# A cross-attention kernel on one core: in the last batch product 4's right sums go ahead of block 12; in the first batch several sums, two pairs of scores and T4 are moved

## The chip, the core and the metric

The kernel runs on one core of one Trainium2 chip. Five engines work side by side, each through its own list of instructions in order: TensorE (PE, the matmuls), VectorE (DVE), ScalarE (ACT), GpSimd (POOL) and SyncE (SP). DMAs are issued from the lists of SP, ACT and POOL; an issue that has to wait for a semaphore stands in its list like any other instruction. The metric is the time of one execution on the device in microseconds (us), lower is better.

## The reference, cut to what matters

Eight batches. In each, x1 and x2 are 512 channels by 1024 positions, all float32:

```python
q = einsum('bcn,dc->bnd', x1, Wq) + bq            # d = 64
k = einsum('bcn,dc->bdn', x2, Wk) + bk[:, None]
v = einsum('bcn,dc->bdn', x2, Wv) + bv[:, None]
attn = softmax(einsum('bnd,bdm->bnm', q, k), axis=2)
out = einsum('bcm,bnm->bcn', v, attn) + x1
```

## The kernel before

**The algebra.** With e the exponentials of the scores less their maximum and den their sums, the output is Wv (x2 e) / den + bv + x1. Per batch the kernel makes Y = x2 e (512 x 1024 times 1024 x 1024), scales it by 1/den, makes Wv Y, and adds bias and x1. Both big products are cut in 2 x 2 blocks and done with seven block products instead of eight. The left factor x2 gives blocks a11, a12, a21, a22 and the left sums S1 (of a21 and a22), S2 (of a11 and S1), S3 (of a11 and a21, written over a21) and S4 (of a12 and S2); the right factor e gives blocks 11, 12, 21, 22 and the right sums T1 (of 12 and 11), T2 (of T1 and 22), T3 (of 22 and 12, written over 12) and T4 (of 21 and T2). The signs stand in `left_sums` (L101) and `right_sums` (L259). The table `MULT` (L298 on) says which factors each product takes: 1: a11 and block 11; 2: a12 and 21; 6: S2 and T2; 7: S3 and T3; 5: S1 and T1; 3: S4 and 22; 4: a22 and T4. Some of the products, 3 and 4 in every batch, are cut in seven once more, by `inner_left` (L349), `inner_right` (L358) and `multiply_onto` (L422); for product 4 the four inner right sums are made by `inner_right(s, 4, ...)`, four VectorE instructions, and the inner products that need them come second and later.

**Tiles.** Positions (the contraction of the first product) lie on the 128 partitions. A right block holds 4 tiles of 128 x 512; query halves 0 and 1 are `s.e[0]` and `s.e[1]`. `scores(s, h, i)` makes one pair of score tiles (one of each half of the keys) for half h, and ScalarE copies them from PSUM to SBUF. Then VectorE folds the maximum over the four pairs (`fold`), GpSimd reduces it over the partitions (`highest`, PARTITION_ALL_REDUCE, top), VectorE subtracts (L243 in the head, L249 elsewhere), ScalarE exponentiates, VectorE folds the sum and GpSimd reduces it (`total`, den). Its reciprocal is taken on a small copy (`few`) and sent back through DRAM (`shares`).

**The order.** It is written out by hand: the program is recorded under a manual schedule, so that each engine's list is in the order of the source. `head` (L609) and `head_second` (L685) are the start of batch 0; `period(s, n, nn, nnn)` (L708) is batch s, with the scores and projections of the next batch n and the loads for the two batches after it woven in. `nn` is the batch after next: in `period` of batch 0 its queries are projected (`queries(nn)`, PE L149 ps_q) right after the scores of half 0 of batch 1.

**The loads on SP.** `load_x` (L122) loads x1 or x2 of a batch in four DMAs of 512 KB into one buffer (tag x). `load_a` (L128) loads a block of x2 transposed; the tiles a11 and a12 have one buffer each, a21 and a22 two (`bufs=1 + (k[0] == "2")`, L131). A load into a buffer waits until the last reader of the tile that lay there is done, and SP issues in the order of the list. In the first batch that list reads, after the loads of the head: x1 of batch 1, x2 of batch 1 (after its queries), a11 of batch 1 (L732), x1 of batch 2 (L737, after the keys of batch 1), a21 and a22 of batch 1, x2 of batch 2. The readers of batch 0's a11 are product 1 on TensorE and the sums S2 and S3 on VectorE.

**The first batch around the change.** `head` makes, in order: the scores of half 0, their maximum; S1 and S2 on VectorE while GpSimd reduces; three pairs of scores of half 1; the eight subtractions and exponentials of half 0; three folds of its sum. `period` runs product 1, then `head_second`: fourth pair, the rest of the maximum of half 1, the queries of batch 1, S3 and S4 while GpSimd reduces, the exponentials of half 1. Then T1 and T2, the reduction of sum 0, product 2, the keys of batch 1, `sum_t4` (L271; in batches 0 and 1 two VectorE additions, from batch 2 on two ScalarE copies and two accumulating DMAs of POOL), the sum of half 1, T3, product 6, the scores and queries that belong to the next batches, products 5, 7, 3, 4.

**The last batch around the change.** After product 7, `multiply_3(s, hooks[1])` makes product 3 onto bank a; `evict_y(s, "22", (1,))` completes block 22; `evict_3()` adds the inner terms and completes block 12 (three VectorE instructions: `complete`, then two additions from PSUM); `inner_right(s, 4, ...)` makes the inner right sums of product 4; then the blocks are scaled by 1/den, and `multiply_4` follows.

Of the kernel before, what the change touches and what calls it, by code (L numbers as in the profile page):

```python
# [11 lines left out]
ALU = mybir.AluOpType  # L12
# [3 lines left out]
def kernel(  # L16
# [53 lines left out]
    MH = N // P // 2  # L70
# [64 lines left out]
    def sum_a(s, *ks):  # L135
        for k in ks:
            if k != "S3":
                s.a[k] = sb.tile([P, MH, C // 2], F32, tag=f"a{k}", name=f"a{k}_{s.b}")
        left_sums(s.a, *ks)
# [35 lines left out]
    def scores(s, h, i, bank=None):  # L175


        if i == 0:
            s.e[h] = sb.tile([P, 2, MH, H], F32, tag=f"e{h}", name=f"e_{s.b}_{h}")
        e = s.e[h]  # L180
        if bank:
            whole = None
            ps = [
                ps_a.tile([P, H], F32, tag=f"{bank}{g}", name=f"ps_s{bank}{g}_{s.b}_{h}_{i}")
                for g in range(2)
            ]
        else:
            whole = ps_s.tile([P, 2, H], F32, tag="sc", name=f"ps_s_{s.b}_{h}_{i}")
            ps = [whole[:, g, :] for g in range(2)]
        for g, r in ((0, lo), (1, hi)):  # L190
            nc.tensor.matmul(  # L191
                ps[g], s.k[r, ts(i, P)], s.q[r, ts(h, H)], start=True, stop=True
            )

        def copy():
            if bank:
                for g in range(2):
                    nc.scalar.copy(e[:, g, i, :], ps[g])
            else:
                nc.scalar.copy(e[:, :, i, :], whole)  # L200

        copy.ps = ps
        return copy

    def fold(s, h, i, kind, op):

        e = s.e[h]
        if i == 1:
            s.mx[h] = sb.tile([P, 2, H], F32, tag="fold", name=f"{kind}_{s.b}_{h}", bufs=2)
        f = s.mx[h]  # L210
        nc.vector.tensor_tensor(f, e[:, :, 0, :] if i == 1 else f, e[:, :, i, :], op)  # L211
# [59 lines left out]
    def sum_t4(s):  # L271

        s.t["T4"] = t4 = sb.tile([P, MH, H], F32, tag="eT4", name=f"eT4_{s.b}")
        if s.b < 2:
            sum_e(s, "T4")
            return
        for i in (0, 2):
            nc.scalar.copy(t4[:, i : i + 2, :], s.t["21"][:, i : i + 2, :])
        for i in (0, 2):
            nc.gpsimd.dma_start(t4[:, i : i + 2, :], s.t["T2"][:, i : i + 2, :], accum_op=ALU.add)  # L280
# [328 lines left out]
    def head(s):  # L609

        s.q = sb.tile([P, N], F32, tag="q", name=f"q_{s.b}", bufs=2)
        s.k = sb.tile([P, H], F32, tag="k", name=f"k_{s.b}", bufs=2)
        x1_sb = sb.tile([P, CT, N], F32, tag="x", name="x1_head")
        x2_sb = sb.tile([P, 2, MH, H], F32, tag="e1", name="x2_head")
        s.x = x2_sb.rearrange("p a (b t) n -> p (a b) (t n)", t=2)  # L620

        def load_x1(c, h):
            nc.sync.dma_start(
                x1_sb[:, c : c + 2, ts(h, H)],
                x1[s.b, c * P : (c + 2) * P, ts(h, H)].rearrange("(t p) n -> p t n", p=P),
            )

        nc.gpsimd.dma_start(bqk_sb, bqk)
        nc.gpsimd.dma_start(bv_sb, bv)
        nc.scalar.dma_start(wqk_sb, wqk)  # L630
        warm = const.tile([P, P], F32, name="warm")
        nc.vector.memset(warm, 0.0)
        ps = ps_a.tile([P, H], F32, tag="a0", name="ps_warm")
        for _ in range(WARM):
            nc.tensor.matmul(ps[:, 0:P], warm, warm, start=True, stop=True)
        load_x1(0, 0)
        load_x1(2, 0)
        for n in HALVES:
            for c in range(CT):
                to, of = (  # L640
                    x.rearrange("p (h n) -> p h n", h=2)[:, :, n]
                    for x in (s.x[:, c, :], x2[s.b, ts(c, P), :])
                )
                nc.sync.dma_start(to, of)
        nc.scalar.activation(warm[:, 0:1], warm[:, 0:1], AF.Exp)
        load_x1(0, 1)
        load_x1(2, 1)
        load_a(s, "21", "22", "11", "12")
        load_values()
        tiles = range(CT)  # L650
        head_queries(s, x1_sb, 0, "c1")(*tiles)
        head_keys(s, left, "c0")(*tiles)
        more_keys = head_keys(s, right, "a0")
        more_keys(0)
        s.mx[0] = f = sb.tile([P, 2, H], F32, tag="fold", name=f"max_{s.b}_0", bufs=2)
        copies = [scores(s, 0, i) for i in range(2)]
        for g in range(2):
            nc.scalar.copy(s.e[0][:, g, 0, :], copies[0].ps[g])
            nc.vector.tensor_tensor(f[:, g, :], s.e[0][:, g, 0, :], copies[1].ps[g], ALU.max)
        fold_halves(s, 0, ALU.max)  # L660
        more_keys(*tiles[1:])
        copies[1]()
        more_queries = head_queries(s, x1_sb, 1)
        more_queries(0)
        for i, bank in ((2, "a"), (3, "c")):
            copy = scores(s, 0, i, bank)
            for g in range(2):
                nc.vector.tensor_tensor(f[:, 0, :], f[:, 0, :], copy.ps[g], ALU.max)
            copy()
        highest(s, 0, halves=False)  # L670
        sum_a(s, "S1", "S2")
        more_queries(*tiles[1:])
        load_x(states[1], x1)
        copies = [scores(s, 1, 0), scores(s, 1, 1), scores(s, 1, 2, "c")]
        for g in range(2):
            for i in range(MH):
                first_exponentials(s, g, i)
        for copy in copies:
            copy()
        fold(s, 0, 1, "sum", ALU.add)  # L680
        fold(s, 0, 2, "sum", ALU.add)
        fold(s, 1, 1, "max", ALU.max)
        fold(s, 0, 3, "sum", ALU.add)

    def head_second(s, n):  # L685


        scores(s, 1, 3)()
        for i in range(2, MH):
            fold(s, 1, i, "max", ALU.max)  # L690
        queries(n)
        load_x(n, x2)
        highest(s, 1)
        sum_a(s, "S3", "S4")
        for i in range(MH):
            exponentials(s, 1, i)

# [10 lines left out]
    def period(s, n, nn, nnn):  # L708
# [15 lines left out]
        if s.b == 0:  # L724
            head_second(s, n)
        sum_e(s, "T1", "T2")
        if s.b < 2:
            total(s, 0)
        else:
            shares(s, 0)  # L730
        if n:
            load_a(n, "11")  # L732
        if s.b == 0:
            first(2)
            evict_y(s, "11", (1,))
            keys(n)
            load_x(nn, x1)  # L737
            sum_t4(s)
            sums(s, 1)
            shares(s, 0)  # L740
        else:
            evict = multiply_2(s)
            sums(s, 1)
            evict()
            if s.b == 1:
                shares(s, 0)
            sum_t4(s)
            sum_a(s, "S4")
# [37 lines left out]
        if seven:  # L786
            hooks = [{}, {}]
            if n:
                for i in range(MH):
                    lower(n, 0, i)  # L790
                hooks = [
                    {
                        1: lambda: copy_first(n, 0),
                        6: lambda: add_exponential(1),
                        5: lambda: add_exponential(2),
                    },
                    {6: lambda: add_exponential(3)},
                ]
            first(5, (lambda: exponential(n, 0, 0)) if n else None)
            inner_right(s, 3, s.t["22"], "eT1")  # L800
            inner_left(s, 4, s.a["22"], "a12")
            add_7 = multiply_7(s, hooks[0])
            add_7()
            evict_3 = multiply_3(s, hooks[1])
            evict_y(s, "22", (1,))
            evict_3()
            inner_right(s, 4, s.t["T4"], "eT2")
        else:
            first(5)
            if s.b == 0:  # L810
                inner_right(s, 3, s.t["22"], "eT1")
                for i in range(MH):
                    lower(n, 0, i)
            else:
                for i in range(MH):
                    exponentials(n, 0, i)
                start_sum(n, 0)
                inner_right(s, 3, s.t["22"], "eT1")
            first(7)
            if s.b > 1:  # L820
                inner_right(s, 4, s.t["T4"], "eT2")
            evict_3 = multiply_3(s, {})
            if s.b:
                evict_y(s, "22", (1,))
                evict_3()
            else:
                evict_3()
                evict_y(s, "22", (1,))
# [105 lines left out]
```

## Time and profile before

| what | value |
|---|---|
| median of 3 runs | 693.22 us (693.14 to 693.31) |
| the profiled execution's own time | 693.62 us |
| its span, first to last instruction | 691.8 us |
| PE busy | 682.8 us, 99% |
| DVE busy | 628.9 us, 91% |
| ACT busy | 276.1 us, 40% |
| POOL busy | 193.5 us, 28% |
| mean DMA rate | 158 GB/s |
| mean granted TensorE clock | 1.000 |

Times inside the execution are counted from the start of the span. A line of the timeline gives the start, the length, the engine, the line of the source, the operation, out<-in, shapes, the number of instructions merged, and in brackets the idle time of the engine before it with what ended it. "SPq", "POOLq" and "ACTq" are issues and waits in an engine's list. A matmul's length includes its pipeline; the distance from one start to the next is what it costs TensorE: 0.43 us for a matmul record of 512 columns, 0.215 us where two column groups of 64 share the array, as in the projections.

### The profile page before, as it was taken

Reading aid. Unit: us, or ns where it says so; the run is one execution under the profiler, and the core shown is the slowest. Engines: PE = TensorE matmul, PEld = TensorE weight load, DVE = VectorE, ACT = ScalarE, POOL = GpSimd, SP = SyncE. Lnnn points to the kernel's source line nnn. Section 1 sums busy time; section 2 is a strip of 40 time slices with the busy share of each in tenths; the row PEclk is TensorE's granted clock in tenths of the full one; section 3 lists DMA queues with packets and bytes.
Section 4 is the critical chain, followed back from the end, with each engine's and each line's share of the span. In section 5 each row is a group of like instructions: output and inputs, shape, how many; then the busy total and the mean of one; then the engine's idle time right before and its main releaser. Section 6 shows DMA issues by size and latency. Waiting matters only on the chain.

```text
span 691.8 us, 6647 instructions
## 1 busy us (share of the span) xinstructions
PE 682.8 (99%) x2248; PEld 364.2 (53%) x2248; DVE 628.9 (91%) x809; ACT 276.1 (40%) x439; POOL 193.5 (28%) x147
## 2 busy tenths in 40 slices
PE   9999999999999999999999999999999999999997
PEld 5333554535545565455644566454754545545753
DVE  1999999988999889998999989999799988999785
ACT  2733353146233552345432454424544245243220
POOL 0123113522423223242142321623223232323000
PEclk9999999999999999999999999999999999999999
DMA  9676256954569754786628867198642864268303
GB/s 304 258 214 238 65 182 130 255 161 79 183 114 235 199 106 153 150 231 181 135 111 180 230 181 187 42 198 215 167 92 38 207 166 76 62 148 223 87 0 122
DMA packets 44723, 109.05 MB, mean 158 GB/s; under 512 B 4880, under 2 KB 7184, under 8 KB 44688
## 3 DMA queue, kind: packets, MB, share of 16 engines
q1 hardware_dynamic: 25856, 70.13, 30.1%
q0 software_dynamic: 17424, 36.25, 29.7%
q10 hardware_dynamic: 1408, 2.23, 1.0%
q8 instruction: 18, 0.29, 0.2%
q14 instruction: 17, 0.14, 0.1%
HBM read 72.62 MB, written 16.81 MB: 129 GB/s over the span
## 4 chain that ended last, share of the span: by engine, by line
PE 93%; DMA 3%; DVE 1%; SPq 1%; ACT 1%; issue 0%; DVEq 0%
PE ps_ya L321 24%; PE ps_i L374 17%; PE ps_oa L321 16%; PE ps_oc L321 12%; PE ps_s L191 6%; PE ps_yc L374 5%; PE ps_q L149 4%; PE ps_k L149 3%; PE ps_yc L321 3%; PE ps_ya L374 3%; DMA a<-in_x2T_dram 1%; DMA x_in_x_dram<-in_x_dram 1%; DMA x_head<-in_x_dram 1%; PE ps_sc L191 1%; PE ps_sa L191 1%; DVE aS L110 0%
## 5 line engine op out<-in xcount | busy, mean ns | idle before, releaser
L321 PE MATMUL ps_ya<-eT,aS 128*128 128x512 f32 x256 | 113.1, 595 | 0.0
L332 ACT COPY uy<-ps_ya 128x512 f32<-128x512 f32 x48 | 28.1, 588 | 139.6 <-PE ps_ya L321 126.7
L249 DVE TENSOR_TENSOR e<-e,top 128x1024 f32<-128x1024 f32 x60 | 70.5, 1228 | 11.0 <-POOL top L221 11.0
L321 PEld LDWEIGHTS ps_ya<-eT,aS 128*128 128x128 f32 x256 | 48.0, 190 | 60.9 <-issue 58.5
L253 ACT ACTIVATE e<-e 128x1024 f32<-128x1024 f32 x60 | 62.9, 1059 | 38.6 <-DVE e L249 37.1
L221 POOL PARTITION_ALL_REDUCE top<-max x16 | 32.8, 2052 | 150.8 <-DVE max L215 78.9
L226 POOL PARTITION_ALL_REDUCE den<-sum x16 | 63.4, 3961 | 40.8 <-DVE sum L215 35.8
L321 PE MATMUL ps_oa<-yT,w_S 128*128 128x512 f32 x128 | 57.6, 593 | 0.0
L321 PE MATMUL ps_oc<-y,w 128*128 128x512 f32 x128 | 57.6, 593 | 0.0
L321 PE MATMUL ps_ya<-e,a 128*128 128x512 f32 x128 | 56.3, 593 | 0.3 <-ACT e L244 0.3
L200 ACT COPY e<-ps_s 128x1024 f32<-128x1024 f32 x46 | 45.7, 1027 | 19.3 <-PE ps_s L191 17.5
L332 ACT COPY uo<-ps_oa 128x512 f32<-128x512 f32 x48 | 27.6, 584 | 54.2 <-PE ps_oa L321 44.9
L383 ACT COPY d<-ps_i 128x256 f32<-128x256 f32 x84 | 29.3, 374 | 47.7 <-PE ps_i L374 47.2
L191 PE MATMUL ps_s<-q,k 64*128 64x512 f32 x188 | 47.3, 608 | 0.8 <-ACT q L590 0.8
L551 POOL DMA_DIRECT2D uo<-in_x_dram x21 | 24.9, 1186 | 79.2 <-DVE uo L548 79.2
L555 POOL DMA_DIRECT2D sum<-e x21 | 25.7, 1222 | 66.5 <-DMA sum<-e 37.0
L321 PEld LDWEIGHTS ps_ya<-e,a 128*128 128x128 f32 x128 | 24.2, 190 | 31.3 <-issue 29.6
L321 PEld LDWEIGHTS ps_oa<-yT,w_S 128*128 128x128 f32 x128 | 24.2, 190 | 30.8 <-issue 29.9
L321 PEld LDWEIGHTS ps_oc<-y,w 128*128 128x128 f32 x128 | 24.1, 190 | 31.0 <-issue 28.9
L211 DVE TENSOR_TENSOR max<-max,e 128x1024 f32<-128x1024 f32 x30 | 36.8, 1225 | 3.0
L507 DVE TENSOR_TENSOR y<-y,den 128x512 f32<-128x512 f32 x54 | 33.8, 683 | 0.0
L238 POOL DMA_DIRECT2D den<-row x16 | 8.9, 557 | 79.0 <-DMA row<-few 73.2
(142 smaller groups left out, 1291.4 us busy)
## 6 DMA issues: line engine op xcount, KB each, us to landing
x_in_x_dram<-in_x_dram SPq DMA_DIRECT2D x60, 512.0 KB, 5.9
a<-in_x2T_dram SPq DMA_DIRECT2D x32, 512.0 KB, 7.1
sum<-e POOLq DMA_DIRECT2D x21, 512.0 KB, 5.2
uo<-in_x_dram POOLq DMA_DIRECT2D x21, 512.0 KB, 6.5
out_dram<-uo SPq DMA_DIRECT2D x21, 512.0 KB, 5.1
eT<-eT POOLq DMA_DIRECT2D x12, 512.0 KB, 6.5
den<-row POOLq DMA_DIRECT2D x16, 256.0 KB, 3.6
r<-in_x_dram POOLq DMA_DIRECT2D x7, 512.0 KB, 8.6
```

The costliest lines, as they stand in the source:

```text
L149: nc.tensor.matmul(ps[r, :], w_sb[:, c, :], s.x[:, c, ts(h, H)], start=(c == 0), stop=(c == CT - 1),)
L191: nc.tensor.matmul(ps[g], s.k[r, ts(i, P)], s.q[r, ts(h, H)], start=True, stop=True)
L200: nc.scalar.copy(e[:, :, i, :], whole)
L211: nc.vector.tensor_tensor(f, e[:, :, 0, :] if i == 1 else f, e[:, :, i, :], op)
L221: nc.gpsimd.partition_all_reduce(s.top[h], s.mx[h][:, 0, :], P, ReduceOp.max)
L226: nc.gpsimd.partition_all_reduce(s.den[h], s.mx[h][:, 0, :], P, ReduceOp.add)
L249: nc.vector.tensor_tensor(e, e, top, ALU.subtract)
L253: nc.scalar.activation(e, e, AF.Exp)
L321: nc.tensor.matmul(ps[:, n], left[ka][:, k, ts(j, P)], right[kb][:, k, n], start=opens and k == 0, stop=i in (2, 3, 4) and k == n_k - 1, s ...
L332: nc.scalar.copy(s.tmp[i][:, j, :], ps)
L374: nc.tensor.matmul(ps, s.inner[i][ka][:, k, :], s.inner[i, "t"][kb][:, k, :], start=opens and k == 0, stop=z in (2, 3, 4) and k == MH // 2 ...
L507: nc.vector.tensor_tensor(y[:, j, :], y[:, j, :], rden, ALU.mult)
```

## The change

In the last batch, and only there, `inner_right(s, 4, ...)` is called before `evict_3()`.

In the first batch:

- pair 2 of the scores of half 1 leaves `head` for `head_second`, so that TensorE makes pairs 2 and 3 after product 1 (in the file before, pair 2 came ahead of it);
- S1 and S2 come after the eight subtractions of half 0 on VectorE, where they came ahead of them;
- S3 and S4 leave `head_second` for `period`, behind `shares(s, 0)`, that is behind the sum of half 1;
- of the three folds of sum 0, the last two go behind T1 and T2;
- T4 is made by two ScalarE copies and two accumulating DMAs of POOL, as in batches 2 to 7, where it was two VectorE additions. Batch 1 keeps the additions.

The source calls `load_a(n, "11")` where it did. No arithmetic is added or left out.

```diff
     def sum_t4(s):
 
         s.t["T4"] = t4 = sb.tile([P, MH, H], F32, tag="eT4", name=f"eT4_{s.b}")
-        if s.b < 2:
+        if s.b == 1:
             sum_e(s, "T4")
             return
         for i in (0, 2):
@@ head
         highest(s, 0, halves=False)
-        sum_a(s, "S1", "S2")
         more_queries(*tiles[1:])
         load_x(states[1], x1)
-        copies = [scores(s, 1, 0), scores(s, 1, 1), scores(s, 1, 2, "c")]
+        copies = [scores(s, 1, i) for i in range(2)]
         for g in range(2):
             for i in range(MH):
                 first_exponentials(s, g, i)
         for copy in copies:
             copy()
+        sum_a(s, "S1", "S2")
+        fold(s, 1, 1, "max", ALU.max)
         fold(s, 0, 1, "sum", ALU.add)
-        fold(s, 0, 2, "sum", ALU.add)
-        fold(s, 1, 1, "max", ALU.max)
-        fold(s, 0, 3, "sum", ALU.add)
 
     def head_second(s, n):
 
-        scores(s, 1, 3)()
+        copies = [scores(s, 1, 2, "c"), scores(s, 1, 3)]
+        for copy in copies:
+            copy()
         for i in range(2, MH):
             fold(s, 1, i, "max", ALU.max)
         queries(n)
         load_x(n, x2)
         highest(s, 1)
-        sum_a(s, "S3", "S4")
         for i in range(MH):
             exponentials(s, 1, i)
@@ period
         sum_e(s, "T1", "T2")
+        if s.b == 0:
+            for i in range(2, MH):
+                fold(s, 0, i, "sum", ALU.add)
         if s.b < 2:
             total(s, 0)
@@
             sum_t4(s)
             sums(s, 1)
             shares(s, 0)
+            sum_a(s, "S3", "S4")
@@
             evict_y(s, "22", (1,))
-            evict_3()
+            if n:
+                evict_3()
             inner_right(s, 4, s.t["T4"], "eT2")
+            if not n:
+                evict_3()
```

## The prediction

> **What bounds the kernel now.** The page comes first, for the bound and the chain that ended last.
>
> ```profile
> PE 682.8 (99%) x2248; PEld 364.2 (53%) x2248; DVE 628.9 (91%) x809; ACT 276.1 (40%) x439; POOL 193.5 (28%) x147
> ...
> PE 93%; DMA 3%; DVE 1%; SPq 1%; ACT 1%; issue 0%; DVEq 0%
> ```
>
> TensorE never rests for long, so a change pays only where TensorE waits, and costs only where it is made to wait. The waits of TensorE come next, the longest two:
>
> ```profile
> PE ps_i L374 <- DVE eI4eT L367: 2.3, 1, 2.3
> ...
> PE ps_s L191 <- ACT q L590: 0.8, 1, 0.8
> ```
>
> The first is in the last batch. The timelines of TensorE and VectorE there show product 4 standing still until its inner right sums (eI4eT) exist, and VectorE making block 12 (L452, L483) ahead of them.
>
> ```profile
> 655.34 1.03 PE L374 MATMUL ps_i<-eT,a 128*128 128x256 f32 x4
> 658.65 1.97 PE L374 MATMUL ps_i<-eI4eT,aI 128*128 128x256 f32 x8 [2.28 <-DVE eI4eT L367]
> ```
>
> ```profile
> 652.31 1.01 DVE L502 TENSOR_TENSOR y<-ps_yc,uy 128x512 f32<-128x512 f32 x2
> 654.49 0.69 DVE L452 TENSOR_TENSOR d<-d,v 128x512 f32<-128x512 f32 x1 [1.16 <-ACT d L383]
> 655.29 1.29 DVE L483 TENSOR_TENSOR y<-ps_ya,d 128x512 f32<-128x512 f32 x2
> 656.49 0.68 DVE L367 TENSOR_TENSOR eI4eT<-eT 128x512 f32<-128x512 f32 x1
> ```
>
> For the first batch I read SP's timeline (x2 of batch 1, a11 of batch 1, x1 of batch 2, a21 and a22), then TensorE at the queries of batch 2, which read that x1, and at product 5 behind them.
>
> ```profile
> 36.78 2.00 SPq L126 DMA_DIRECT2D x_in_x_dram<-in_x_dram  x4
> 38.82 0.78 SPq L133 DMA_DIRECT2D a<-in_x2T_dram  x1
> 48.00 1.75 SPq L126 DMA_DIRECT2D x_in_x_dram<-in_x_dram  x4
> 49.79 1.22 SPq L133 DMA_DIRECT2D a<-in_x2T_dram  x2
> ```
>
> ```profile
> 58.58 3.65 PE L149 MATMUL ps_q<-x_in_x_dram,wqk_sb 128*64 128x512 f32 x16
> 62.17 1.12 PE L321 MATMUL ps_ya<-eT,aS 128*128 128x512 f32 x2
> ```
>
> Last come VectorE and GpSimd, for the sums that move and the reductions beside them.
>
> ```profile
> 36.44 1.22 DVE L110 TENSOR_TENSOR a<-a,a 128x1024 f32<-128x1024 f32 x1
> 37.58 2.06 DVE L110 TENSOR_TENSOR aS<-a,aS 128x1024 f32<-128x1024 f32 x1
> 39.56 4.62 DVE L249 TENSOR_TENSOR e<-e,top 128x1024 f32<-128x1024 f32 x4
> ...
> 50.69 3.44 DVE L262 TENSOR_TENSOR eT<-e,eT 128x1024 f32<-128x1024 f32 x2
> ...
> 58.51 4.38 DVE L262 TENSOR_TENSOR e<-e 128x1024 f32<-128x1024 f32 x2
> ```
>
> ```profile
> 20.63 2.68 POOL L221 PARTITION_ALL_REDUCE top<-max  x1 [18.15 <-DVE max L668]
> ```
>
> ```profile
> 152.81 1.78 POOL L221 PARTITION_ALL_REDUCE top<-max  x1 [11.20 <-DVE few L234]
> ```
>
> S3 is the first line: done at 37.66, before a11's issue at 38.82. A reduction beside VectorE's 128x1024 sums takes 2.68, with VectorE idle 1.78, and it holds up one sum (2.06 for S4, 3.44 where two take 2.4).
>
> **The change part by part.** *Last batch.* The four inner sums can start when block 22's evictions end, at 653.3 (T4 landed long before). They take 0.69, 0.72, 0.61 and 0.61 (start to start); the third, which the second inner product needs, ends at 655.25. TensorE reaches that product at 655.34 + 0.86 = 656.2 and does not wait. It started at 658.65: 2.45 gained. Late next is VectorE's block 12: its three instructions start at 655.8 and end at 657.85, and the 1.24 between 659.02 and 657.78 is what VectorE gains down to block 21, scaled by 669.19 - 1.24 = 667.95; its reader, at 670.77 on TensorE, comes to 668.32. So it fits by 0.37; if not, some tenths come back. Term: -2.45 (0 if the stall only changes its name).
>
> *Scores, S1 and S2 later.* The first top reduction then runs with VectorE idle: 20.63 + 1.78 = 22.41, VectorE starts at 22.45 instead of 23.57, and product 1 at 23.84 instead of 24.96 (the 1.39 for a subtraction and an exponential kept). But the third pair, 0.86, now follows product 1 instead of filling the wait for it, so the queries of batch 1 start at 33.08 - 1.12 + 0.86 = 32.82: 0.26 earlier. x2 of batch 1 is issued when they end, so the keys and product 6 come 0.26 earlier too (47.63). S1 and S2, 2.4 behind the subtractions, end at 29.7, hidden behind product 1, whose next reader of S2 is product 6. Copies of pairs 2 and 3 on ScalarE end at 32.8 and 33.96, the maximum at 36.1; the second reduction, again alone, ends at 36.2 + 1.78 = 37.97, and the subtractions start at 38.0 instead of 39.56.
>
> *T4 on ScalarE and POOL.* Two copies (1.99 in batch 7's row) fit between the keys' activation at 48.4 and product 6's first copy at 51.4. The two DMAs stand in POOL's list behind few_0 (54.7 to 56.6 by batch 7's 1.80 for two) and ahead of the second sum's reduction (57.2): nobody waits. They land by 62 (4.6 to 6.5 us after issue in quiet stretches); the first reader is inner_right, after 65. If that cover went, product 4's 89.36 is the next limit. VectorE loses 3.36 of work (50.69 to 54.05).
>
> *Sums later, and S3.* VectorE from 38.0: subtractions, T1 and T2 take 9.33 (39.56 to 48.89), to 47.3; two folds of sum 0, 2.5, and halves, 0.7, to 50.5; block 11, 1.2, to 51.7; the first fold of sum 1 is held by the den reduction (3.24, from 50.6) to 53.9; two folds, halves and the reciprocal, 3.3, to 57.2. few_0, issued at 54.2, lands by 56.5 at its median of 2.3 us. S3 then takes 1.2: done at 58.4 instead of 37.66. T3 follows S4 and ends near 63, before product 7 (76 before).
>
> *What stands behind S3.* a11 of batch 1 overwrites the a11 that S3 reads, in its only buffer. In the built program that load waits for VectorE's 42nd signal, which is S3 (26th before, S3 again). SP issues in order, so behind it stand x1 of batch 2 (four DMAs), a21, a22. The queries of batch 2 need that x1 at 58.3, where it was issued at 48.0 and had all landed by 55.8 (the fourth issued at 49.32, landed 6.5 later). Now: a11 issued at 58.4, x1 right behind. Five loads land, by that row, the first 3.8 after issue, the fifth 1.3 after the fourth's 7.8: 9.1, so 67.5. The T4 DMAs may still be running (61.8): between 0 and 2.2 more (x2 of batch 2, issued at 62.28 beside other transfers, took 10.05 for its four instead of 7.8); 0.6 taken. Product 5 follows the last landing by 1.0 (the keys' last chunk at 46.88, product 6 at 47.88): 69.1.
>
> *The clock.* TensorE would stand from 58.3 to about 63.8. The only row of an idle TensorE is the end of the run:
>
> ```profile
> 691.60:691.80 0.20, 0.00 (x0) 0.00 (x0) 0.00 (x0) 0.00 (x0) 0.00 (x0) 0.50 0.00 0
> ```
>
> The granted clock is 0.50 there, 3.5 us after the last matmul, and the first 20 matmuls of the run (128 columns) came 0.213 us apart, as far as 256-column records stand apart later, for 4.3 us. At half speed for 4.3 us from 63.8, ten of the 16 records take 0.43 and six 0.215: 5.6 us instead of the 4.8 that the landings allow: 0.8 more. If the clock holds, 0. I take 0.4. (The Trainium skill, TensorE: Matmul & The Clock Gate, Part 1, says that the gate halves the clock after an idle window of about 3.4 us and opens after about 3.4 us of work; by it eight records are slow, 5.2 us, an estimate, 0.4 more and not 0.8. No run here shows yet which.)
>
> Sum: product 5 at 69.1 + 0.4 = 69.5 instead of 62.17, +7.3; it holds the 0.26 gained earlier. After 62 the trace shows no wait of TensorE that could give this back until 586, and that one is VectorE's, which moves along. 7.3 - 2.45 = +4.9 on the profiled execution's 693.62 (span 691.8 and 1.8 around it), which lies 0.40 above the median: 693.22 + 4.9 = 698.1.
>
> **The rivals.**
> 1. *S3 is later still.* The reduction of sum 1 starts when S3 does; T3's second half beside such a reduction took 3.26, not 1.2: +2.1. Or few_0 lands 5.9 us after issue, as its slowest did, and holds the reciprocal to 60.1: +2.9. Against: T3's first half, in just S3's place behind the reciprocal, took 1.19. 700.2 to 701.
> 2. *The loads are quicker or partly covered.* No contention, clock held, S3 0.5 earlier: 7.3 - 0.6 - 0.4 - 0.5 = 5.8, less 2.45: 696.6, and down to 695.8 if the chunks land closer together.
> 3. *SP's hold ends too early to matter: faster.* Then the last batch's 2.45 and the 0.26 remain: 690.5. Product 5 must start by 62.17 + 2.45 = 64.6 for break-even, so S3 must be done by 64.6 - 10.1 = 54.5, 3.9 before my chain. For: T4's 3.36 left VectorE. Against: it is counted already, and two folds took its place.
> 4. *The last batch gains nothing*: block 21 or the denominators become the wait. 698.1 + 2.45 = 700.5. Against: the 0.37 of room.
>
> **How the numbers follow.** My forecast 0.60 (own range 696.9 to 699.5); rival 1 0.17; rival 2 0.12; rival 3 0.05; rival 4 0.06. The predicted time is 698.1. A range from 696.4 to 700.8 leaves out rival 3, the lower half of rival 2 and the far part of rival 1, about 0.18. Within 0.2% (1.4 us, about what a measurement can tell from no change) there is only a rival 3 that half works: 0.02. Faster 0.05, slower 0.93.
>
> **What would show it.** Right: a wait of 5 to 6 us of ps_q L149 on x_in_x_dram near 58 and smaller ones between its chunks; SP's a11 issue near 58.4; S3 there on VectorE; both top reductions at about 1.78; product 5 near 69.5; no eI4eT wait of 2.3 in the last batch; a granted clock under 1 near 63 if it falls. Wrong: SP's x1 issue still at 48, or product 5 near 62.

## The result and the profile after

The changed kernel takes **701.17 us** (median of 6 executions, 700.86 to 701.85). The kernel before, run on the same chip, took 694.35 (693.14 to 697.17, 6 executions), so the ratio is 1.0098, with a 95% interval of 1.0083 to 1.0114: about 1% slower. The profiled execution took 700.86, its span is 699.1, its mean granted clock 0.995. Against the span of before (691.8) that is +7.3, where the prediction had +4.9. Executions of the kernel before lie in two groups, 693.1 to 693.8 and 694.9 to 695.7 (one took 697.17), and the last experiment is about that.

On the page TensorE's share has fallen from 99% to 98%, and in the chain that ended last PE went from 93% to 91% while VectorE went from 1% to 4%.

```profile
span 699.1 us, 6655 instructions
...
PE 683.6 (98%) x2248; PEld 363.9 (52%) x2248; DVE 626.8 (90%) x807; ACT 278.0 (40%) x441; POOL 190.1 (27%) x149
...
PE 91%; DVE 4%; DMA 2%; POOL 1%; ACT 0%; SPq 0%; issue 0%; DVEq 0%
```

The longest waits of TensorE after (us in total, times, the longest):

```profile
PE ps_q L149 <- DMA x_in_x_dram<-in_x_dram: 8.4, 2, 7.9
PE ps_q L586 <- DMA x_head<-in_x_dram: 1.2, 1, 1.2
...
PE ps_s L191 <- ACT q L590: 0.8, 1, 0.8
```

The wait of 2.3 for eI4eT is gone, and 8.4 in two waits has come: the queries of batch 2 wait for their x1. SP's timeline after shows why. a11 of batch 1 (L133) is issued at 58.77, where it was 38.82 (among SP's waits this issue stands 20.3 for S3, VectorE's L110), and the four loads of x1 stand behind it, at 59.27 instead of 48.00:

```profile
36.50 2.00 SPq L126 DMA_DIRECT2D x_in_x_dram<-in_x_dram  x4
58.77 0.33 SPq L133 DMA_DIRECT2D a<-in_x2T_dram  x1
59.27 3.09 SPq L126 DMA_DIRECT2D x_in_x_dram<-in_x_dram  x4
62.41 1.13 SPq L133 DMA_DIRECT2D a<-in_x2T_dram  x2
```

TensorE's timeline after, from the queries of batch 2 (58.58 before) to product 5 (62.17 before):

```profile
66.10 4.11 PE L149 MATMUL ps_q<-x_in_x_dram,wqk_sb 128*64 128x512 f32 x12 [7.89 <-DMA x_in_x_dram<-in_x_dram]
70.74 1.08 PE L149 MATMUL ps_q<-x_in_x_dram,wqk_sb 128*64 128x512 f32 x4 [0.53 <-DMA x_in_x_dram<-in_x_dram]
71.75 1.55 PE L321 MATMUL ps_ya<-eT,aS 128*128 128x512 f32 x3
```

The chain that ended last, cut to this stretch (start, length, what), goes from the sum of half 1 through the reciprocal (L234) and S3 (L110) on VectorE to SP's issues and the last landing:

```profile
56.85 0.69 DVE sum L215
57.54 0.09 DVE few L234
57.63 1.12 DVE a L110
...
58.77 0.33 SPq L133
...
59.27 1.07 SPq L126
...
60.39 0.76 SPq L126
...
61.19 0.55 SPq L126
...
61.78 8.92 DMA x_in_x_dram<-in_x_dram
...
70.74 1.08 PE ps_q L149 x4
```

Two things in it go beyond the prediction: the issues took 1.07, 0.76 and 0.55 instead of some 0.43, and the last load took 8.92 to land, where the last of the four took 6.5 before. The windows there (busy time of PE, PEld, DVE, ACT, POOL, then the granted clock, the DMA share and GB/s) show full DMA engines and half clock together:

```profile
62.00:66.00 4.00, 0.00 (x0) 0.00 (x0) 3.90 (x4) 0.00 (x0) 1.14 (x2) 0.50 0.94 352
66.00:70.00 4.00, 3.90 (x12) 1.09 (x12) 3.83 (x5) 0.00 (x0) 1.50 (x2) 0.65 1.05 403
```

Product 5 starts 9.58 later than before; TensorE keeps that distance, 9.6 to 9.8, until the last batch, and there 2.45 come back. The two lines of product 4 that stood at 655.34 and 658.65 before, with 2.28 of waiting between them, now follow each other without a wait:

```profile
665.11 1.03 PE L374 MATMUL ps_i<-eT,a 128*128 128x256 f32 x4
665.97 1.89 PE L374 MATMUL ps_i<-eI4eT,aI 128*128 128x256 f32 x8
```

### The profile page after: what moved, and what is told of

It is laid out like the page before. It is cut to its first block, busy times and chain, and to the rows that moved or that the text cites. A ratio compares the mean times of both kernels' runs of the same rounds, so it can differ in the third digit from the quotient of the medians.

```text
span 699.1 us, 6655 instructions
## 1 busy us (share of the span) xinstructions
PE 683.6 (98%) x2248; PEld 363.9 (52%) x2248; DVE 626.8 (90%) x807; ACT 278.0 (40%) x441; POOL 190.1 (27%) x149
## 3 DMA queue, kind: packets, MB, share of 16 engines
q10 hardware_dynamic: 1408, 2.23, 1.0%
## 4 chain that ended last, share of the span: by engine, by line
PE 91%; DVE 4%; DMA 2%; POOL 1%; ACT 0%; SPq 0%; issue 0%; DVEq 0%
PE ps_ya L321 23%; PE ps_i L374 17%; PE ps_oa L321 16%; PE ps_oc L321 12%; PE ps_s L191 5%; PE ps_yc L374 5%; PE ps_k L149 3%; PE ps_ya L374 3%; PE ps_yc L321 3%; PE ps_q L149 3%; DMA x_in_x_dram<-in_x_dram 1%; DVE sum L211 1%; PE ps_sa L191 1%; PE ps_sc L191 1%; DMA x_head<-in_x_dram 1%; DVE eT L262 1%
## 5 line engine op out<-in xcount | busy, mean ns | idle before, releaser
L221 POOL PARTITION_ALL_REDUCE top<-max x16 | 31.1, 1941 | 155.1 <-DVE max L215 83.3
L226 POOL PARTITION_ALL_REDUCE den<-sum x16 | 59.7, 3729 | 39.0 <-DVE sum L215 38.1
L200 ACT COPY e<-ps_s 128x1024 f32<-128x1024 f32 x46 | 45.7, 1028 | 19.1 <-PE ps_s L191 17.3
L149 PE MATMUL ps_q<-x_in_x_dram,wqk_sb 128*64 128x512 f32 x112 | 27.1, 625 | 8.4 <-DMA x_in_x_dram<-in_x_dram 8.4
```

Of the source, the lines that this page charges most:

```text
L149: nc.tensor.matmul(ps[r, :], w_sb[:, c, :], s.x[:, c, ts(h, H)], start=(c == 0), stop=(c == CT - 1),)
L221: nc.gpsimd.partition_all_reduce(s.top[h], s.mx[h][:, 0, :], P, ReduceOp.max)
L226: nc.gpsimd.partition_all_reduce(s.den[h], s.mx[h][:, 0, :], P, ReduceOp.add)
```

## The experiments

**The last batch alone.** The kernel before with only this:

```diff
             evict_y(s, "22", (1,))
-            evict_3()
+            if n:
+                evict_3()
             inner_right(s, 4, s.t["T4"], "eT2")
+            if not n:
+                evict_3()
```

> The change's last-batch part alone, the first batch as before. Theory (SP's hold behind S3 makes the loss, the last batch's 2.45 us are a gain of their own): the eI4eT wait of 2.3 us is gone, 2.4 us under the kernel before, ratio 0.9965. Rival (the wait only changes its place, to block 21 or a denominator): the eI4eT wait goes, another of 1 to 2.4 us stands in the last 40 us, ratio 0.998 to 1.000.

Measured: 691.08 (690.70 to 691.17, 4 executions) against 695.02 for the kernel before (8 executions beside it, 693.33 to 695.47): ratio 0.9947 [0.9928, 0.9966]. Its span is 689.4, 2.4 below the profile of before, and TensorE's second part of product 4 starts 2.41 earlier. Its longest waits are now those of the head, and none has taken the place of eI4eT:

```profile
PE ps_warm L635 <- DVE warm L632: 1.0, 1, 1.0
PE ps_s L191 <- ACT q L590: 0.8, 1, 0.8
```

This half of the change is a plain gain. The two medians differ by 3.9 and not by 2.4 since five of the eight executions of before are of its longer group; against the other three (693.33 to 693.61) the gain is 2.3 to 2.5. The last experiment takes that up.

**S3 and S4 late, alone.** The kernel before with the other suspected cause and nothing else; T4 stays on VectorE and the last batch as it was:

```diff
@@ head_second
-        sum_a(s, "S3", "S4")
@@ period
             shares(s, 0)
+            sum_a(s, "S3", "S4")
```

> The kernel before with one part of the change alone: S3 and S4 behind the sum of half 1. T4 stays on VectorE, the last batch is as before. Theory (the hold on SP alone makes the loss): S3 ends near 58.7, a11 of batch 1 is issued there, the four loads of x1 of batch 2 land from 5 to 9 us later (no T4 DMAs beside them: last at 67.8), product 5 near 69; 6.6 us over the kernel before, ratio 1.0095. Rival (the loss comes from the other moved sums, the scores or T4's DMAs): product 5 within 1 us of 62, ratio within 0.002 of 1.

Measured: 701.79 (701.47 to 702.56, 4 executions), ratio 1.0104 [1.0087, 1.0122], span 699.8. Moving these two sums brings by itself most of the loss, 7.6 of the 9.6 at product 5. That the time is as long as the changed kernel's comes from the last batch, whose wait of 2.3 this kernel keeps. SP's timeline and TensorE's waits of this kernel:

```profile
58.59 0.33 SPq L133 DMA_DIRECT2D a<-in_x2T_dram  x1
59.09 1.96 SPq L126 DMA_DIRECT2D x_in_x_dram<-in_x_dram  x4
```

```profile
PE ps_q L149 <- DMA x_in_x_dram<-in_x_dram: 5.8, 3, 5.0
PE ps_i L374 <- DVE eI4eT L367: 2.3, 1, 2.3
```

a11 landed 3.50 after its issue and the last chunk of x1 10.11 after it, and product 5 started at 69.76, 7.6 later than before. That is over the expectation, again because the loads landed later than by the row used.

**S3 and S4 back.** The opposite: the changed kernel with only these two sums where they were.

```diff
@@ head_second
         highest(s, 1)
+        sum_a(s, "S3", "S4")
@@ period
             shares(s, 0)
-            sum_a(s, "S3", "S4")
```

> The changed kernel with S3 and S4 alone put back beside the second maximum's reduction. Theory (hold): a11 is issued near 38.5 again, no wait of the queries of batch 2, product 5 near 61.9; with the last batch's gain 2.7 us under the kernel before, ratio 0.996. Rival (the other moves of the first batch cost as well): TensorE still waits more than 1 us between 45 and 80, ratio 0.999 or more.

Measured: 691.18 (690.90 to 691.45, 4 executions), ratio 0.995 [0.9934, 0.9966], span 689.5. SP's timeline is that of before:

```profile
38.78 0.68 SPq L133 DMA_DIRECT2D a<-in_x2T_dram  x1
47.74 1.75 SPq L126 DMA_DIRECT2D x_in_x_dram<-in_x_dram  x4
```

So the other four moves of the first batch (scores, S1 and S2, folds of sum 0, T4) neither gain nor cost anything that a median shows: 691.18 beside 691.08 without them. Product 6 and the queries of batch 2 do come 0.25 earlier than before (47.63 and 58.33), and a small wait for eI3eT (0.2) gives most of that back.

**S3 late, but x1 ahead of a11.** The changed kernel, with the load of a11 in the first batch issued behind x1 of batch 2, so that S3 holds only a11, a21 and a22:

```diff
-        if n:
+        if s.b and n:
             load_a(n, "11")
@@
             load_x(nn, x1)
+            load_a(n, "11")
```

> The changed kernel with one load in another place of SP's list: in the first batch a11 of batch 1 is issued behind x1 of batch 2 instead of ahead of it. S3 stays late. Theory (what costs is what stands behind a11 on SP, not S3's lateness): x1 is issued near 47.6 and has landed by 55.5, a11 itself still waits until 58.7, product 5 near 61.9; 2.8 us under the kernel before, ratio 0.996. Rival (S3, S4 and the sums before them are too late for VectorE's own readers, or a21 and a22 behind a11 come too late): waits of TensorE for VectorE or for a21 after 62, ratio above 0.998.

Measured: 692.00 (691.70 to 692.34, 5 executions), ratio 0.9965 [0.9950, 0.9979], span 690.3.

```profile
36.86 12.76 SPq L126 DMA_DIRECT2D x_in_x_dram<-in_x_dram  x8
59.13 3.29 SPq L133 DMA_DIRECT2D a<-in_x2T_dram  x3
```

```profile
PE ps_i L374 <- DVE eI3eT L367: 0.8, 1, 0.8
```

a11 still waits for S3 (59.13), but x1 no longer stands behind it, and the wait of the queries is gone. The hold in SP's order is the cause, then, and not a late a11. The second fence is what stands behind it: with S3 and S4 late, VectorE makes the inner sums of product 3 0.8 too late. In the changed kernel the wait for x1 covers that.

**T4 on VectorE.** The landings took 11.9 in the changed kernel and 10.1 in the one with S3 and S4 late alone, whose T4 has no DMAs. Here the changed kernel makes T4 with its two VectorE additions, behind S3 and S4:

```diff
-        if s.b == 1:
+        if s.b < 2:
             sum_e(s, "T4")
@@ period, first batch
-            sum_t4(s)
             sums(s, 1)
             shares(s, 0)
             sum_a(s, "S3", "S4")
+            sum_t4(s)
```

> The changed kernel with T4 of the first batch on VectorE, behind S3 and S4, so that no DMA of T4 runs beside the held loads; S3 stays where it is. It prices the term that the prediction put at 0.6 us (T4's DMAs beside the five loads). Theory (T4's DMAs made the five loads slower): a11 is issued near 58.7 and lands 3.5 us later instead of 5.9, the last x1 lands 10.1 after a11's issue as with S3 late alone (11.9 in the changed kernel), product 5 near 69.9 instead of 71.75. Rival (the loads are slow in this place anyway): last x1 11.5 to 12 after a11's issue, product 5 near 71.7.

Measured: 701.95 (one execution), span 700.2. The landings did what was expected: a11 landed 3.21 after its issue at 59.18, the last x1 9.79 after it, at 68.98. The time did not follow, since another wait came in: the scores of batch 1 are copied over block 21 of e, which T4 on VectorE now still reads (ScalarE's copy, L200, waits 9.4 for VectorE's L262).

```profile
65.76 2.08 PE L191 MATMUL ps_s<-q,k 64*128 64x512 f32 x4 [8.31 <-ACT e L200]
67.77 5.39 PE L149 MATMUL ps_q<-x_in_x_dram,wqk_sb 128*64 128x512 f32 x16
```

The expected time was missed (product 5 at 73.10), so this run says something of the landings and nothing of what they are worth.

**T4's DMAs later.** To get that, the ScalarE copies of T4 stay, and only its two DMAs are issued behind the first maximum of batch 1; the inner right sums of product 4, which read T4, go behind product 7:

```diff
         for i in (0, 2):
             nc.scalar.copy(t4[:, i : i + 2, :], s.t["21"][:, i : i + 2, :])
+        if s.b:
+            add_t4(s)
+
+    def add_t4(s):
+
+        t4 = s.t["T4"]
         for i in (0, 2):
             nc.gpsimd.dma_start(t4[:, i : i + 2, :], s.t["T2"][:, i : i + 2, :], accum_op=ALU.add)
@@ period, behind highest(n, 0)
         if s.b == 0:
+            add_t4(s)
             inner_left(s, 4, s.a["22"], "a12")
-            inner_right(s, 4, s.t["T4"], "eT2")
             inner_left(s, 3, s.a["S4"], "aI3")
@@
             first(7)
-            if s.b > 1:
+            if s.b != 1:
                 inner_right(s, 4, s.t["T4"], "eT2")
```

> The changed kernel with only the two accumulating DMAs of T4 in the first batch issued later, behind the first maximum of batch 1 (after 70 us instead of at 55), and the four inner right sums of product 4 that read T4 made behind product 7 instead of ahead of it; the ScalarE copies stay. Theory (T4's DMAs lengthen the landings of x1 by about 2.1, the rest of the over-run lies in the hold): a11 issued at 58.8, first landing 3.2 to 3.6 later, last x1 landing at 68.6 to 68.9 instead of 70.70, product 5 at 69.6 to 69.9 instead of 71.75, and nothing takes it back, so 699.1 us against 701.2. Rival (T4's DMAs don't slow the loads; the landings in the run with T4 on VectorE were short for another reason): last landing 70.7, product 5 at 71.7, 701.2 us.

Measured: 699.48 (699.31 to 700.72, 4 executions; 693.82 for the kernel before beside it, ratio 1.0082 [1.0061, 1.0103]). The median is 1.7 below the changed kernel's, the span, 697.8, 1.3 below. The group of the four x1 loads, from issue to landing, first for the changed kernel and then with T4's DMAs late:

```profile
L126 SPq DMA_DIRECT2D x_in_x_dram<-in_x_dram x4: 553/671/1069, 59.3 to 61.8; - x4
...
DMA to landing us min/median/max: 6.7/7.3/8.9
```

```profile
L126 SPq DMA_DIRECT2D x_in_x_dram<-in_x_dram x4: 328/431/449, 59.7 to 61.0; - x4
...
DMA to landing us min/median/max: 4.1/6.5/7.7
```

The first line of each has the length of an issue in ns (minimum, median, maximum): with T4's DMAs running, SP's issues themselves are slower. a11 landed 3.33 after its issue instead of 5.91, the last x1 9.54 instead of 11.93. So T4's DMAs, issued at 55.07 and 55.63 and landed at 59.62 and 63.38, cost these loads 2.4. Not all of it reaches product 5, which starts at 70.23, 1.52 earlier; TensorE's timeline of this kernel shows why:

```profile
63.89 1.98 PE L149 MATMUL ps_q<-x_in_x_dram,wqk_sb 128*64 128x512 f32 x4 [5.46 <-DMA x_in_x_dram<-in_x_dram]
66.15 4.15 PE L149 MATMUL ps_q<-x_in_x_dram,wqk_sb 128*64 128x512 f32 x12 [0.29 <-DMA x_in_x_dram<-in_x_dram]
70.23 7.13 PE L327 MATMUL ps_ya<-eT,aS 128*128 128x512 f32 x16
```

The last twelve records run without a pause, at half clock to 68.9, and end 1.52 after the last landing (68.71) instead of 1.05: here the clock costs 0.47. S3 is also 0.40 later than in the changed kernel, which goes back to the loads of the head (SP's issues there took longer in this execution).

**The clock kept up.** The changed kernel with 34 spare matmuls of 128 columns (their result is not read) ahead of the queries of batch 2, so that TensorE doesn't rest:

```diff
+            if s.b == 0:
+                ps = ps_s.tile([P, 2, H], F32, tag="sc", name="ps_keep")[:, 0, :]
+                for _ in range(34):
+                    nc.tensor.matmul(ps[:, 0:P], s.warm, s.warm, start=True, stop=True)
```

> The changed kernel with 34 matmuls of 128 columns on a spare tile, result unread, put on TensorE ahead of the queries of batch 2, where it would stand idle from 58.0 to 66.1: the granted clock should stay at 1.00 there. Theory A (the half clock costs nothing, since the last x1's landing sets the end): product 5 again 1.05 us after the last x1 landing, within 0.2 us of 71.75. Theory B (the half clock costs 0.4 us or more, as the prediction's term had it): product 5 at 71.3 or earlier with the landings unchanged.

Measured: 701.24 (one execution), span 699.5, granted clock 1.00 from 5.6 to 698.5.

The spare matmuls leave two records each:

```profile
58.13 7.86 PE L775 MATMUL ps_keep<-warm 128*128 128x128 f32 x68
...
71.26 1.08 PE L149 MATMUL ps_q<-x_in_x_dram,wqk_sb 128*64 128x512 f32 x4 [0.99 <-DMA x_in_x_dram<-in_x_dram]
72.27 3.27 PE L321 MATMUL ps_ya<-eT,aS 128*128 128x512 f32 x7
```

The last x1 landed at 71.21 and product 5 came 1.06 after it, as in the changed kernel (1.05 at half clock). The half clock cost the changed kernel nothing, because the records of the first three loads were done 0.53 before the last load had landed (0.99 before it at full clock). The start itself was 0.5 later than expected, with the landing.

**Two groups of the kernel before.** The kernel before was profiled four times more, for an execution of its longer group.

> The kernel before itself, for a profile of one of its longer executions: its runs lie in two groups, 693.3 to 693.6 us with a granted clock of 0.999 to 1.000 and 694.9 to 695.5 with 0.997 to 0.998. Theory (the wait of 2.3 us for eI4eT in the last batch lets the clock fall to half for one stretch of 3.4 us in some executions, 1.7 us each): in an execution of the longer group the half clock stands right behind that wait, near 659 to 663. Rival: it stands in the first 60 us, at the loads, and has nothing to do with the change.

> The same as the other look at the kernel before, taken again because which group an execution falls in is not chosen: half clock right behind the eI4eT wait (theory) or among the first batch's waits for loads (rival), if this one is of the longer group; if it is of the shorter one, no half clock between 6 and 690 us.

> The kernel before, one look, to catch an execution of its longer group (694.9 to 695.5 us). Theory: such an execution shows one stretch of 3.4 us at a granted clock of 0.50, at the last batch's wait for the inner right sums (655 to 662). Rival: the stretch lies elsewhere, or the execution is long without one. An execution of the shorter group (693.2 to 693.6) shows no such stretch and decides nothing.

> The same as the look before it: a long execution with a stretch of 3.4 us at half clock at 655 to 662 (theory), elsewhere or none (rival); a short one decides nothing.

The first three took 693.29, 693.21 and 693.82, all of the shorter group. The fourth took 695.22 (span 693.4). TensorE and the windows of this execution around product 4's wait:

```profile
655.25 1.03 PE L374 MATMUL ps_i<-eT,a 128*128 128x256 f32 x4
658.56 3.45 PE L374 MATMUL ps_i<-eI4eT,aI 128*128 128x256 f32 x8 [2.28 <-DVE eI4eT L367]
661.80 1.27 PE L374 MATMUL ps_yc<-eT,a 128*128 128x256 f32 x4
```

```profile
657.00:658.90 1.90, 0.34 (x2) 0.35 (x3) 1.86 (x4) 0.00 (x0) 0.00 (x0) 0.99 0.02 4
658.90:662.30 3.40, 3.40 (x10) 2.65 (x9) 3.40 (x8) 0.63 (x2) 0.00 (x0) 0.50 0.00 0
662.30:665.00 2.70, 2.70 (x14) 2.39 (x13) 2.67 (x4) 0.76 (x3) 0.00 (x0) 1.00 0.00 0
```

The eight records take 3.45 here and 1.97 in the profile shown of before: right after the wait for eI4eT the clock stands at 0.50 for 3.4 us, which costs 1.7 where TensorE is the limit. The third of the four has the same wait and full clock. So in this longer execution the extra time lies at that wait. For the other long ones (but not for the single 697.17, which stays unexplained) it is inferred: where a mean clock is given it is 0.997 or 0.998, one such stretch, and the 13 executions of the three kernels without this wait and without a hold of 7 us (the last batch alone, S3 and S4 back, a11 behind x1) have 0.999 or 1.000. Against the shorter group alone (693.14 to 693.31 beside it) the changed kernel is some 7.9 longer, not 6.8. The last-batch reorder is worth 2.4, and 1.7 more whenever the clock would have fallen. (The Trainium skill, TensorE: Matmul & The Clock Gate, Part 1, says that the clock falls after at least one idle window of about 3.4 us, and that the window runs free of the program. That the fall comes in some executions only agrees with a window that runs free; but here 2.28 of waiting were enough, less than the page asks for.)

## Why the prediction was right in kind and short in size

The direction, the place and the mechanism came out as written; the forecast of 698.1 was 3.1 short, and the range, 696.4 to 700.8, ended 0.4 below the measured 701.17. By the prediction's steps:

- *Last batch, −2.45 with 0.37 of room.* Right: the distance to before falls from +9.77 to +7.32 at that place, no wait follows, and the run with this alone confirms it. Rival 4 falls.
- *Scores, S1 and S2 later.* Right: the reductions take 1.78 with VectorE idle, the queries of batch 1 end 0.28 earlier (0.26 predicted), the subtractions start at 38.34 (38.0).
- *S3 at 58.4.* Measured 58.74, a11's issue at 58.77: +0.37. The small part of rival 1 that came true: T1, T2 and the sums end a few tenths later, while few_0 landed in 2.0. The rival's own upper figure, 701, meets the measured time by luck: its cause, few_0 landing late, did not come. T3 behind S4 was called covered, and the inner sums of product 3 behind it were not priced. The wait for x1 covers both; with that wait gone the inner sums cost 0.8.
- *a11 holds x1, a21 and a22.* Right, and shown from both sides: S3 and S4 late alone gives 7.6 of the 9.6, S3 and S4 back removes all of it, x1 ahead of a11 all but the 0.8 of another wait. Rival 3 falls.
- *Five loads land 9.1 after a11's issue, and T4's DMAs add 0.6.* **This is the step that failed.** Measured 11.93 instead of 9.7: +2.23. The mis-sized term is above all the 0.6 for T4's DMAs, "between 0 and 2.2": with them out of the way the landings take 9.54 (T4's DMAs late), 9.79 (T4 on VectorE) and 10.11 (S3 and S4 late alone), so they cost 1.8 to 2.4, about the upper end of the bound. The choice near the lower end rested on both DMAs having landed by 62, from landings of 4.6 to 6.5; the row that these come from goes up to 10.6, the second DMA took 7.75 and landed at 63.38, and beside it even the issues on SP slowed down, for which the sum had no term. The 9.1 itself was 0.4 to 1.0 low by the same three runs; why is open.
- *Product 5 = last landing + 1.0 + 0.4 for the clock.* Measured 1.05 in all: −0.35. The clock did fall, to 0.50 from 61.96 to 68.79; 2.7 of that lay under the queries, which started at 66.10, where the sum had 4.3, and the late last landing hid it. The 4.3 was the start of one execution: in the profile after, the first matmuls turn to full speed after 2.9, at 3.94. The 0.4 belongs to the case with quicker landings: 0.47 in the run with T4's DMAs late.

Together 0.37 + 2.23 − 0.35 = 2.25, and product 5 stands at 71.75 instead of 69.5. Clock and contention were added as independent terms, but they cover one another: in the changed kernel the late landing hides the clock, and with T4's DMAs late the clock takes back 0.47 of the 2.4.

These steps alone would give some 700.4, still inside the range. About 0.1 more came up between product 5 and the end, and about 0.7 is no step at all but the choice of executions: the sum started from a profile that lay 0.40 above its median, and the profiled execution after, 700.86, is the shortest of its six and lies 0.31 below theirs. Why the others are longer is not shown; three of them have a mean clock of 0.992 instead of 0.995. The range had no room for either: it had no bound above 9.1 for the landings without T4's DMAs, and none for the spread of executions.

Neither half of the change is needed for the other. The best of these kernels are the last-batch reorder alone (691.08) and the changed kernel with S3 and S4 back (691.18). Giving a11 a second buffer, which would free S3's place altogether, wasn't tried.

## What to carry to other kernels

Before moving an operation later, look for what it reads: if it is the last reader of a single buffer, its end becomes the issue time of the next load, and of everything behind that load in the same issuing list. If such a sum must be late, move the load behind what it would hold; this brought 9 us back here. And when several loads start at once, price transfers that are already running at the upper end of the bound, issue times included; here they cost 1.8 to 2.4.

## What the runs showed of the hardware that I had not expected

- DMAs that run beside a burst slow its issue too: SP's issues of x1 took 0.55 to 1.07 us beside T4's accumulating DMAs and 0.33 to 0.45 with these DMAs later, and the first landing (a11) came 5.91 instead of 3.33 after its issue.
- A wait of TensorE of 2.28 us was enough for half clock in one profiled execution of the kernel before and not in others; the stretch at half clock is 3.41 us there and with S3 and S4 late alone, 6.83, twice as much, in the changed kernel, and 10.24, three times as much, with T4 on VectorE.
- Half clock costs nothing where landings set the pace (1.05 from the last landing to product 5 at half clock, 1.06 at full clock), 0.47 where the last landing came 2.4 sooner after a11's issue, and 1.7 in a stretch of 3.4 us that TensorE alone sets.
